# A kernel of four graph layers: q copied to PSUM a block ahead, and layer 0's count of places read one step later

## The chip, the cores and the metric

The kernel runs on one core of one Trainium2 chip. The core has a matrix engine (TensorE, "PE" in the profile; its weight loads are "PEld"), a vector engine (VectorE, "DVE"), a scalar engine (ScalarE, "ACT"), a general engine (GpSimd, "POOL"), a queue engine (SyncE, "SP") and 16 DMA engines. Each engine runs its own instructions in order and waits for others by semaphores. Tiles lie in SBUF, or in PSUM, which the matrix engine writes.

The metric is the device time of one execution in microseconds (us). Several runs are taken, and their median counts.

## The reference, cut to what matters

There are 3327 nodes with 256 features and a 0/1 matrix `adj` of 3327 x 3327, which is sparse: an entry is 1 with probability 0.0048, so that a node has some 16 neighbours. Layer 0 weighs neighbours and the others with a softmax whose scores take only two values in a row. Layers 1 to 3 are attention over the neighbours, each followed by an MLP.

```python
# layer 0
h = x @ Wt.T + bt                                  # 64 features
s = leaky_relu(h @ Wa.T + ba, negative_slope=0.2)
w = softmax(where(adj > 0, s, NEG), axis=1)
y = x + (w @ h) @ Wp.T + bp
x = gamma * (y - mean(y)) * rsqrt(var(y) + EPS) + beta

# layers 1, 2, 3
qkv = layer_norm(x, g1, be1) @ w_qkv               # q, k, v: 8 heads of 32
scores = einsum("nhd,mhd->hnm", q, k) * SCALE
attn = softmax(where(adj != 0, scores, -inf), axis=-1)
x = x + einsum("hnm,mhd->nhd", attn, v).reshape(n, 256) @ w_proj + b_proj
x = x + gelu(layer_norm(x, g2, be2) @ w1 + b1) @ w2 + b2
```

## The kernel before

**Layer 0** goes over `adj` in 26 blocks of 128 rows. Per block it loads the rows, takes the sign (ACT), turns them with PE (ACT copies the turned tiles out of PSUM), sums the neighbours' features with PE, and finds the list of neighbours of each row with DVE (`candidates`, `list`). Rows come in groups of four blocks. When a group's sums are there, its steps run spread over the following blocks: `soft`, then `mix`, `project` and so on.

The kernel sorts the nodes by their degree. For this, `soft` makes a one-hot row `OH` of each node's degree and lets PE count, into the PSUM tile `places`, how many earlier nodes have the same degree; DVE reads the count back into `rank`:

```python
def soft(self):
    ...                                            # deg from the group's sums
    nc.vector.tensor_tensor(OH[:, b0:b0 + n, :], ..., ALU.is_equal)
    at = places[:, :4 * nd].rearrange("p (b k) -> p b k", k=nd)
    for j in range(n):
        ...
        nc.tensor.matmul(at[:, j, :], lhsT, OH[:, m, :], start=False, stop=True, ...)
    t = aw.tile([P, 4, nd], FP, tag="place", ...)
    nc.vector.tensor_mul(t, at[:, :n, :], OH[:, b0:b0 + n, :])          # L906
    nc.vector.tensor_reduce(rank[:, b0:b0 + n], t, AX.X, ALU.add)       # L907
    if b0 + n == NB:
        nc.tensor.matmul(at[:, n - 1, :], rest_tri, OH[:, NB - 1, :], ...)
        S.all = at[:, n - 1, :]
    ...                                            # twelve small DVE operations
    nc.scalar.activation(m1, m1, AF.Exp)
    nc.scalar.activation(m0, m0, AF.Exp)

def mix(self):
    ...                                            # uses m1, m0; ten DVE operations
    nc.vector.tensor_add(nb, nb, t3)
```

After `soft` of a group, `list` of the current block follows, and `mix` comes at the start of the next block, before its `candidates`.

**Layers 1 to 3** work on the sorted nodes, again 26 blocks of 128. `CAPS[b]` is the most neighbours that a node of block `b` may have (40 down to 10). The blocks are taken in the order 25, 1, 24, 2, ..., 12, 13, 0. The neighbours of a block are gathered in groups of four (`GS = 4`): for each of the four, one indirect DMA brings the k and v rows of 128 nodes to a tile of a ring of ten (`kv`, L1298, issued by POOL). DVE multiplies k by q and sums over each head (`scores`), takes softmax, and multiplies v by the weights (`vw`, L1361); PE sums these over the neighbours in PSUM (`po`, L1366). A tile of the ring is free again after its `vw`.

```python
q2 = ps_q.tile([P, 2, D], FP, name="q2")           # PSUM; D = 256, float32

def take_q(self, b):
    self.q[b] = q2[:, ORDER.index(b) % 2, :]
    nc.scalar.copy(self.q[b], t2[:, b, D:2 * D])                        # L1306

def scores(self, b, s0):
    ...
    nc.vector.tensor_mul(k, k, self.q[b][:, None, :].to_broadcast(...)) # L1320
    nc.vector.tensor_reduce(self.sc[b][:, s0:s0 + n, :], ..., ALU.add)  # L1321
    if L == 1:
        nc.scalar.copy(t2[...], t[:, :n, 2 * D])                        # L1324

def softmax(self, b):
    nc.vector.tensor_tensor_reduce(sc, sc, pad[b]..., mx)               # L1332
    nc.scalar.activation(sc, sc, AF.Exp, bias=mx, scale=-1.0)           # L1335
```

The rest of a layer is cut in small steps, which `some()` issues one or a few at a time between the groups. `short` steps finish a block: copy `o`, turn it, copy `oT` (L1396), project (PE, L1402), add to the row (`t`, DVE, L1406) and its statistics. `long` steps work on a chunk of up to four blocks: norm (DVE, then ACT L588, PE L591, ACT L596), the MLP's `up` (PE, L1445), `gelu` (ACT, L1451) and `down` (PE, L1468), `shift` (ACT, L1474), turning back (PE, L1482), add (DVE, L1486), and in layers 1 and 2 the next layer's q, k and v (PE, L1498), copied out by ACT (`kvr`, L1504, and `t`, L1505).

```python
self.take_q(ORDER[0])
for k, b in enumerate(ORDER):
    for g in slots[b]:                             # the groups of block b
        self.scores(*g)
        if g == slots[b][-1]:
            self.softmax(b)
            if k + 1 < NB:
                self.take_q(ORDER[k + 1])
        for i in wait:
            wait[i] += 1
        for _ in range(2 if len(todo) > NBUF // 2 or b == 0 else 1):
            if todo and wait[todo[0][0]] > 1:
                value()                            # weights once per block; vw; po
        self.some()
    todo += slots[b]
    wait[b] = 0
```

The weights and values of a block thus begin two groups after its softmax.

Of the kernel before, what the change touches and what calls it, by code (L numbers as in the profile page):

```python
# [8 lines left out]
FP = mybir.dt.float32  # L9
# [3 lines left out]
ALU = mybir.AluOpType  # L13
AX = mybir.AxisListType
# [3 lines left out]
P = 128  # L18
# [14 lines left out]
NB = (N + P - 1) // P  # L33
# [490 lines left out]
def sparse_path(ctx, tc, ins, out, dram, flag):  # L524
    nc = tc.nc
# [13 lines left out]
    rank = const.tile([P, NB], FP, name="rank")  # L539
# [83 lines left out]
    with tc.tile_pool(name="a", bufs=1) as a, tc.tile_pool(name="aw", bufs=2) as aw, \  # L623
# [45 lines left out]
        for name, n in (("gamma", D), ("beta", D), ("bt", H0), ("Wa", H0), ("ba", 1)):  # L669
# [10 lines left out]
        nd = LMAX + 1  # L680
# [3 lines left out]
        OH = a.tile([P, NB, nd], BF, name="OH")  # L684
        rest_tri = a.tile([P, P], BF, name="rest_tri")
        nc.vector.tensor_sub(rest_tri, ones_bf, tri)

        places = a_acc.tile([P, 512], FP, tag="places", name="places")
# [3 lines left out]
                         skip_group_check=True)  # L692
# [148 lines left out]
        class Group:  # L841
# [36 lines left out]
            def soft(self):  # L878


                g, n, b0 = self.g, self.n, self.blocks[0]

                def sv(name):
                    t = aw.tile([P, 4], FP, tag="s_" + name, bufs=1, name=f"s_{name}_{g}")
                    return t[:, :n]

                sg = S.s[:, b0:b0 + n]
                dg = deg[:, b0:b0 + n]
                nc.vector.tensor_copy(dg, self.acc[:, :n, H0])
                top = sv("top")  # L890
                nc.vector.tensor_scalar(top, dg, float(LMAX), None, ALU.min)
                nc.vector.tensor_tensor(OH[:, b0:b0 + n, :],
                                        num[:, None, :nd].to_broadcast([P, n, nd]),
                                        top[:, :, None].to_broadcast([P, n, nd]), ALU.is_equal)

                at = places[:, :4 * nd].rearrange("p (b k) -> p b k", k=nd)
                for j in range(n):
                    i = b0 + j
                    add = [(tri, i)] + [(ones_bf, k) for k in range(b0, i)]
                    if g:  # L900
                        add += [(rest_tri, i - 4)] + [(ones_bf, k) for k in range(i - 3, b0)]
                    for lhsT, m in add:
                        nc.tensor.matmul(at[:, j, :], lhsT, OH[:, m, :], start=False, stop=True,
                                         skip_group_check=True)
                t = aw.tile([P, 4, nd], FP, tag="place", bufs=1, name=f"place_{g}")[:, :n]
                nc.vector.tensor_mul(t, at[:, :n, :], OH[:, b0:b0 + n, :])  # L906
                nc.vector.tensor_reduce(rank[:, b0:b0 + n], t, AX.X, ALU.add)  # L907
                if b0 + n == NB:
                    nc.tensor.matmul(at[:, n - 1, :], rest_tri, OH[:, NB - 1, :], start=False,
                                     stop=True, skip_group_check=True)  # L910
                    S.all = at[:, n - 1, :]
                non, ga, fa, m1, m0, tt, mx = (
                    sv(k) for k in ("non", "ga", "fa", "m1", "m0", "tt", "mx"))
                nc.vector.tensor_scalar(non, dg, -1.0, float(N), ALU.mult, ALU.add)
                nc.vector.tensor_scalar(ga, dg, 0.0, None, ALU.is_gt)
                nc.vector.tensor_scalar(fa, non, 0.0, None, ALU.is_gt)
                nc.vector.tensor_scalar(tt, ga, -NEG0, NEG0, ALU.mult, ALU.add)
                nc.vector.tensor_mul(m1, sg, ga)
                nc.vector.tensor_add(m1, m1, tt)
                nc.vector.tensor_scalar(tt, fa, -1.0, 1.0, ALU.mult, ALU.add)  # L920
                nc.vector.tensor_mul(m0, sg, tt)
                nc.vector.scalar_tensor_tensor(m0, fa, NEG0, m0, ALU.mult, ALU.add)
                nc.vector.tensor_max(mx, m1, m0)
                nc.vector.tensor_sub(m1, m1, mx)
                nc.vector.tensor_sub(m0, m0, mx)
                nc.scalar.activation(m1, m1, AF.Exp)
                nc.scalar.activation(m0, m0, AF.Exp)
                self.non, self.m1, self.m0, self.tt = non, m1, m0, tt

            def mix(self):  # L930
                g, n, b0, acc = self.g, self.n, self.blocks[0], self.acc
                m1, m0, tt = self.m1, self.m0, self.tt
                z = aw.tile([P, 4], FP, tag="s_z", bufs=1, name=f"s_z_{g}")[:, :n]
                nc.vector.tensor_mul(z, deg[:, b0:b0 + n], m1)
                nc.vector.tensor_mul(tt, self.non, m0)
                nc.vector.tensor_add(z, z, tt)
                nc.vector.reciprocal(z, z)
                nc.vector.tensor_mul(m1, m1, z)
                nc.vector.tensor_mul(m0, m0, z)
                shape = [P, n, H0]  # L940
                nb = self.nb = aw.tile([P, 4, H0], FP, tag="nb", bufs=1, name=f"s_nb_{g}")[:, :n]
                t3 = aw.tile([P, 4, H0], FP, tag="t3", bufs=1, name=f"s_t3_{g}")[:, :n]
                nc.vector.tensor_sub(t3, S.hsum[:, None, :].to_broadcast(shape), acc[:, :n, :H0])
                nc.vector.tensor_mul(t3, t3, m0[:, :, None].to_broadcast(shape))
                nc.vector.tensor_mul(nb, acc[:, :n, :H0], m1[:, :, None].to_broadcast(shape))
                nc.vector.tensor_add(nb, nb, t3)

            def project(self):
                g, n = self.g, self.n
                pt = bank(f"s_ptn_{g}")  # L950
                for j in range(n):
                    nc.tensor.transpose(pt[:H0, j * P:(j + 1) * P], self.nb[:, j, :], ident)
                nc.scalar.copy(S.nT[:H0, :n * P], pt[:H0, :n * P])
                self.ps = []
                for j0 in range(0, n, 2):
                    ps = bank(f"s_pp_{g}_{j0}").rearrange("p (b d) -> p b d", d=D)
                    for j in range(2):
                        nc.tensor.matmul(ps[:, j, :], S.nT[:, (j0 + j) * P:(j0 + j + 1) * P], S.wpT,
                                         start=True, stop=True)
                    self.ps.append(ps)  # L960
# [120 lines left out]
        for g in reversed(range(NG)):  # L1081
            at = dict(zip(names, (0, 1, 3, 4, 5, 6, 7, 8, 9, 10, 11, 12)))
# [11 lines left out]
            for name in names:  # L1094
                k = first + at[name]
# [39 lines left out]
        t = aw.tile([P, NB, nd], FP, tag="v", name="t_more")  # L1135
# [36 lines left out]
        for i in range(NB):  # L1172
            nc.tensor.matmul(pp[:, :2 * NB], oh_lo[:, i, :],
                             ids[:, i, :, :].rearrange("p a b -> p (a b)"),
                             start=(i == 0), stop=(i == NB - 1))
# [87 lines left out]
    ORDER = [b for k in range(NB // 2) for b in (NB - 1 - k, k + 1)][:NB - 1] + [0]  # L1263
    CHUNK, at = {}, 0
# [5 lines left out]
    slots = {b: [(b, s) for s in range(0, CAPS[b], GS)] for b in ORDER}  # L1270

    class Layer:
# [289 lines left out]
        def run(self):  # L1562
            for _ in range(NBUF):
                self.issue()
            self.take_q(ORDER[0])

            todo, wait = [], {}

            def value():
                if todo[0][1] == 0:  # L1570
                    self.weights(todo[0][0])
                self.values(*todo.pop(0))

            for k, b in enumerate(ORDER):
                for g in slots[b]:
                    self.scores(*g)
                    if g == slots[b][-1]:
                        self.softmax(b)
                        if k + 1 < NB:
                            self.take_q(ORDER[k + 1])  # L1580
                    for i in wait:
                        wait[i] += 1
                    for _ in range(2 if len(todo) > NBUF // 2 or b == 0 else 1):
                        if todo and wait[todo[0][0]] > 1:
                            value()
# [3 lines that stand above are left out]
            while todo:  # L1589
                value()  # L1590
                self.some()
            self.rate = 4.0
            while self.short or self.long:
                self.some()
# [45 lines left out]
```

## Time and profile before

The median of three runs is 2787.56 us (2777.72 to 2789.45). The profiled execution has a span of 2779.3 us, and PE was granted 0.836 of its full clock on the mean.

| engine | busy us | share of the span | instructions |
|---|---|---|---|
| PE | 1952.0 | 70% | 6409 |
| PEld | 1045.3 | 38% | 6409 |
| DVE | 1961.9 | 71% | 4061 |
| ACT | 806.5 | 29% | 1398 |
| POOL | 1361.8 | 49% | 1458 |

Layer 0 ends near 525 us, where the first gather of layer 1 is issued. The gathers of layer 1 are issued from 525.0 to 1179.7 us, those of layer 2 from 1303.5 to 1952.5, those of layer 3 from 2074.6 to 2683.3. POOL issues one of them every 1.25 us when it waits for nothing (0.95 us busy, 0.30 between).

A line of the list of waits names who waited, at which line of the kernel and for which tile, then the engine, tile and line that released it, then the total of the waits, their number and the longest. A line of the timeline gives the start and length of an instruction, its engine and line, what it writes and reads, and in brackets how long the engine had been idle before it and what ended that.

### The profile page before, as it was taken

The numbers are of one execution on the slowest core, as the hardware profiler recorded it, in microseconds if no ns is written. First come the engines' busy times: TensorE is split into PE (matmuls) and PEld (weight loads), VectorE is DVE, ScalarE is ACT, GpSimd is POOL, SyncE is SP. The second block draws the span as 40 slices with busy tenths as digits, with TensorE's granted clock in tenths as the row PEclk, the third lists the DMA queues.
The fourth block names the chain that finished last, engine by engine and source line by source line (L and its number), as shares of the span: only waits on it lengthen the run. The fifth ranks groups of instructions, "written<-read, shape, count | busy, mean of one in ns | idle before, by whom it ended". The sixth has DMA issues, their size and how long they took to land. (4 is left out here: it accounts for less than half of the span.)

```text
span 2779.3 us, 21889 instructions
## 1 busy us (share of the span) xinstructions
PE 1952.0 (70%) x6409; PEld 1045.3 (38%) x6409; DVE 1961.9 (71%) x4061; ACT 806.5 (29%) x1398; POOL 1361.8 (49%) x1458
## 2 busy tenths in 40 slices
PE   5657665248788887884377887887853678867866
PEld 4546553114333333442133443433431333333334
DVE  6597888577877777733788677778427878778852
ACT  5346552102332322321022332232320222222221
POOL 4000000377766666601776565566017777776741
PEclk9768776678899898897788898898976898988988
DMA  6224420677766666613776565566227766666650
GB/s 235 99 106 154 155 81 32 198 217 217 222 196 200 202 182 186 182 34 100 209 211 201 168 195 180 158 190 178 50 70 210 210 183 199 201 190 184 198 130 15
DMA packets 144478, 453.66 MB, mean 163 GB/s; under 512 B 29521, under 2 KB 40156, under 8 KB 141021
## 3 DMA queue, kind: packets, MB, share of 16 engines
q0 software_dynamic: 113056, 370.26, 46.0%
q1 hardware_dynamic: 9834, 53.90, 5.5%
q10 hardware_dynamic: 21458, 28.02, 2.9%
q8 instruction: 52, 0.85, 0.1%
q14 instruction: 78, 0.64, 0.1%
HBM read 420.64 MB, written 31.42 MB: 163 GB/s over the span
## 5 line engine op out<-in xcount | busy, mean ns | idle before, releaser
L1298 POOL DMA_INDIRECT kv<-kv,t x1344 | 1272.8, 947 | 810.0 <-issue 350.4
L1366 PE MATMUL po<-vw,s_ident 128*128 128x512 f32 (+1 forms) x1380 | 770.4, 694 | 497.4 <-DVE vw L1361 447.6
L1320 DVE TENSOR_TENSOR kv<-kv,q 128x1024 f32<-128x1024 f32 (+3 forms) x363 | 413.3, 1139 | 312.6 <-ACT q L1306 156.5
L1366 PEld LDWEIGHTS po<-vw,s_ident 128*128 128x128 f32 x1380 | 285.3, 220 | 846.5 <-issue 468.3
L1321 DVE TENSOR_REDUCE sc<-kv 128x32 f32<-128x1024 f32 (+3 forms) x363 | 414.1, 1141 | 12.4
L1361 DVE TENSOR_TENSOR vw<-kv,w 128x1024 f32<-128x1024 f32 x333 | 371.3, 1127 | 0.2
L1445 PE MATMUL pu<-fT,s_w 128*128 128x512 f32 (+3 forms) x768 | 308.1, 536 | 1.0 <-ACT fT L596 1.0
L1468 PE MATMUL py<-gT,s_w 128*128 128x512 f32 (+2 forms) x672 | 283.4, 549 | 0.0
L1451 ACT ACTIVATE gT<-pu,pvb 128x512 f32<-128x512 f32 (+3 forms) x192 | 116.4, 607 | 361.0 <-PE pu L1445 360.7
L1445 PEld LDWEIGHTS pu<-fT,s_w 128*128 128x128 f32 x768 | 150.6, 206 | 140.5 <-issue 116.0
L711 POOL MEMSET s_abf<- 128x1 bf16 x23 | 2.2, 105 | 375.2 <-DVE s_v L731 248.3
L1468 PEld LDWEIGHTS py<-gT,s_w 128*128 128x128 f32 x672 | 127.6, 191 | 122.0 <-issue 104.4
L723 PE MATMUL s_ptb<-s_ident_bf,s_abf 128*128 128x128 bf16 x676 | 69.8, 273 | 77.3 <-ACT s_abf L714 64.0
L735 DVE MAX8 cand<-s_v 128x8 f32<-128x208 bf16 x416 | 118.0, 359 | 0.9
L588 ACT ACTIVATE xn_f<-t,nm_f,rqy_f 128x256 f32<-128x256 f32 x78 | 42.9, 593 | 247.5 <-DVE nm_f L582 240.1
L1498 PE MATMUL pk<-s_w_qkv,nT 128*128 128x512 f32 x208 | 104.4, 626 | 8.9 <-ACT nT L596 8.9
L1335 ACT ACTIVATE sc<-sc,mx 128x120 f32<-128x120 f32 (+6 forms) x78 | 32.0, 410 | 259.8 <-DVE mx L1332 259.2
L1406 DVE TENSOR_TENSOR t<-t,po 128x256 f32<-128x256 f32 x78 | 32.5, 417 | 103.8 <-PE po L1402 97.9
L1486 DVE TENSOR_TENSOR t<-t,pd 128x256 f32<-128x256 f32 x75 | 29.5, 408 | 91.0 <-PE pd L1482 91.0
L723 PEld LDWEIGHTS <-s_abf 128*128 128x128 bf16 x676 | 58.8, 125 | 91.8 <-ACT s_abf L714 70.8
L855 PE MATMUL s_pa<-s_aT,s_hs 128*128 128x256 bf16 x338 | 80.4, 286 | 13.2 <-DVE s_hs L817 13.2
L724 ACT COPY s_aT<-s_ptb 128x896 bf16<-128x896 bf16 x104 | 82.7, 859 | 19.9 <-PE s_ptb L723 19.7
(292 smaller groups left out, 2343.5 us busy)
## 6 DMA issues: line engine op xcount, KB each, us to landing
s_a<-in_adj_dram SPq DMA_DIRECT2D x25, 1663.5 KB
kv<-kv,t POOLq DMA_INDIRECT x1344, 3.7
kv<-kvr ACTq DMA_DIRECT2D x52, 256.0 KB
kv<-s_kvr ACTq DMA_DIRECT2D x26, 256.0 KB
s_w<-in_L_gnn_w_dram SPq DMA_DIRECT2D x6, 1024.0 KB
t<-ql ACTq DMA_DIRECT2D x6, 592.0 KB
t<-s_x ACTq DMA_DIRECT2D x6, 512.0 KB
s_w_qkv<-in_L_gnn_w_qkv_dram SPq DMA_DIRECT2D x3, 768.0 KB
```

Source lines behind the costliest of these rows:

```text
L723: nc.tensor.transpose(pt[:, m, :], self.abf[:, k * P:(k + 1) * P], ident_bf)
L724: nc.scalar.copy(aT[:, k0:k0 + len(ks), :], pt[:, :len(ks), :])
L735: nc.vector.max(out=self.cand[:, s, :], in_=self.v[:, s, :])
L1298: nc.gpsimd.indirect_dma_start(out=t[:, s, :], out_offset=None, in_=kv[L], in_offset=bass.IndirectOffsetOnAxis(ap=t2[:, b, k:k + 1].bitcas ...
L1320: nc.vector.tensor_mul(k, k, self.q[b][:, None, :].to_broadcast([P, n, D]))
L1321: nc.vector.tensor_reduce(self.sc[b][:, s0:s0 + n, :], k.rearrange("p s (h d) -> p s h d", d=HD), AX.X, ALU.add)
L1361: nc.vector.tensor_mul(vw[:, :n * D].rearrange("p (s h d) -> p s h d", h=HEADS, d=HD), v, self.wp[b][:, s0:s0 + n, :, None].to_broadcast([ ...
L1366: nc.tensor.matmul(self.po[b][:, :m], ident, vw[:, s * D:s * D + m], start=(s0 + s == 0), stop=(s0 + s + 2 >= S), skip_group_check=True)
L1445: nc.tensor.matmul(c["pu", f][:, :n], w["w1"][:, e, f * P:(f + 1) * P], c["hT"][:, e, :n], start=(e == 0), stop=(e == 1))
L1451: nc.scalar.activation(g[:, :n], c.pop(("pu", f))[:, :n], AF.Gelu_apprx_tanh, bias=w["b1"][:, f:f + 1])
L1468: nc.tensor.matmul(c["py"][e][:, :n], w["w2"][:, f, e * P:(e + 1) * P], g[:, :n], start=(f == 0), stop=last)
L1498: nc.tensor.matmul(ps[:, :c1 - c0], c["hT"][:, e, j * P:(j + 1) * P], nxt["w_qkv"][:, e, c0:c1], start=(e == 0), stop=(e == 1))
```

## The change

Two things move; no operation is added or taken away.

The copy of the next block's q to PSUM stood after the softmax of the current block. It now stands before the second group of the current block. q2 has two halves, which blocks use in turn, so that the copy for the next block goes to the half that the current block doesn't read. The aim is that q is there long before the next block's first group.

In layer 0, reading the count of places, with the last block's extra matmul, moves from `soft` to the end of `mix`. The aim is that DVE does other work while PE counts.

```diff
@@ soft
-                t = aw.tile([P, 4, nd], FP, tag="place", bufs=1, name=f"place_{g}")[:, :n]
-                nc.vector.tensor_mul(t, at[:, :n, :], OH[:, b0:b0 + n, :])
-                nc.vector.tensor_reduce(rank[:, b0:b0 + n], t, AX.X, ALU.add)
-                if b0 + n == NB:
-                    nc.tensor.matmul(at[:, n - 1, :], rest_tri, OH[:, NB - 1, :], start=False,
-                                     stop=True, skip_group_check=True)
-                    S.all = at[:, n - 1, :]
@@ a new step
+            def place(self):
+                g, n, b0 = self.g, self.n, self.blocks[0]
+                at = places[:, :4 * nd].rearrange("p (b k) -> p b k", k=nd)
+                ...                                # the lines taken out of soft
@@ mix
                 nc.vector.tensor_add(nb, nb, t3)
+                self.place()
@@ run
             for k, b in enumerate(ORDER):
                 for g in slots[b]:
+                    if g == slots[b][1] and k + 1 < NB:
+                        self.take_q(ORDER[k + 1])
                     self.scores(*g)
                     if g == slots[b][-1]:
                         self.softmax(b)
-                        if k + 1 < NB:
-                            self.take_q(ORDER[k + 1])
```

More of the change, by code (lines that the diff above doesn't have):

```diff
@@ L928, in soft @@
                 self.non, self.m1, self.m0, self.tt = non, m1, m0, tt
+            def place(self):
+                g, n, b0 = self.g, self.n, self.blocks[0]
+                at = places[:, :4 * nd].rearrange("p (b k) -> p b k", k=nd)
+                t = aw.tile([P, 4, nd], FP, tag="place", bufs=1, name=f"place_{g}")[:, :n]
+                nc.vector.tensor_mul(t, at[:, :n, :], OH[:, b0:b0 + n, :])
+                nc.vector.tensor_reduce(rank[:, b0:b0 + n], t, AX.X, ALU.add)
+                if b0 + n == NB:
+                    nc.tensor.matmul(at[:, n - 1, :], rest_tri, OH[:, NB - 1, :], start=False,
+                                     stop=True, skip_group_check=True)
+                    S.all = at[:, n - 1, :]
             def mix(self):
```

## The prediction, made before the changed kernel ran

> **What bounds the kernel now.** I read the chain of waits first. Its shares add up to under 10% of the span, so it covers too little to rank stages, and I went on to the list of all waits, then to the stretches where the waits in question lie. Of the list of waits (who waits, for whom; us in total, times, longest) these rows carry the case:
>
> ```profile
> PE po L1366 <- DVE vw L1361: 447.6, 137, 35.0
> ...
> DVE kv L1320 <- ACT q L1306: 156.5, 42, 7.3
> DVE kv L1320 <- DMA kv<-kv,t: 147.0, 67, 6.9
> ...
> POOL kv L1298 <- DVE vw L1361: 102.4, 43, 9.4
> ...
> DVE place L906 <- PE places L903: 41.1, 7, 16.2
> ```
>
> VectorE (DVE) waits 156.5 us for the copy of q and 41.1 us for the count of places. These are the two waits that the change attacks. Whether they are worth anything is a question of stage, so I asked for busy time by stretch (length, then each engine's busy us):
>
> ```profile
> 100.00:300.00 200.00, 131.99 (x886) 102.97 (x884) 148.95 (x542) 108.76 (x130) 1.01 (x10) 0.74 0.36 127
> 300.00:460.00 160.00, 109.47 (x744) 83.10 (x742) 141.35 (x520) 79.38 (x106) 3.68 (x9) 0.78 0.31 102
> 1591.00:1693.00 102.00, 83.25 (x215) 39.34 (x215) 76.41 (x132) 30.28 (x52) 62.03 (x66) 0.90 0.59 177
> ```
>
> Layer 0 (first two rows; columns PE, PEld, DVE, ACT, POOL): from 100 to 460 us DVE is busy 290 of 360 us, and its gaps above 0.25 us there add up to 59 us, 41 of them the wait for places. DVE sets the pace of that stage. Layers 1 and 2 (third row, one turn of four blocks in layer 2): PE 83, DVE 76, POOL 62 of 102 us. No engine is full. DVE works while PE is short of work, then PE works through a backlog (MLP and next layer's qkv) while DVE waits; the turn is the sum of both phases. Layer 3 has turns of 92 us, as it has no qkv.
>
> How one such wait arises (timeline of layer 2, block 19's first group; start, length, engine, line):
>
> ```profile
> 1590.23 0.36 ACT L1306 COPY q<-t 128x256 f32<-128x256 f32 x1
> ...
> 1590.62 1.22 DVE L1320 TENSOR_TENSOR kv<-kv,q 128x1024 f32<-128x1024 f32 x1 [5.95 <-ACT q L1306]
> ...
> 1593.02 0.41 DVE L1406 TENSOR_TENSOR t<-t,po 128x256 f32<-128x256 f32 x1
> ...
> 1594.10 1.22 DVE L1320 TENSOR_TENSOR kv<-kv,q 128x1024 f32<-128x1024 f32 x1
> ...
> 1597.16 0.39 ACT L1505 ACTIVATE t<-pq 128x256 f32<-128x256 f32 x1 [0.28 <-PE pq L1498]
> ...
> 1599.03 0.94 POOL L1298 DMA_INDIRECT kv<-kv,t  x1 [9.39 <-DVE vw L1361]
> ```
>
> The copy takes 0.36 us; the 5.95 us before it is ScalarE (ACT) being late, since everything it runs in order waits for PE's backlog (that list: ACT gT waits 360.7 us for PE pu). So q is a place where DVE is tied to ACT, and the question is where the tie lies afterwards.
>
> **What the skill says.** "PSUM — Partial Sum Buffer", section "PSUM bank collisions raise a hardware error": two engines must not touch one bank in the same partitions at once, even at different addresses, so PSUM is to be guarded by bank. Its specification gives 2 KiB per bank. q2 is 2 x 256 float32, 2048 bytes: both halves are in one bank. In the instruction order of the built kernel this is what stands: ACT's copy for the next block now waits for the multiply of the current block's first group, and the multiply of its second group waits for that copy, though it reads the other half. The same page, "Engine vs sequencer instructions": the queues of ScalarE and VectorE are strictly first in, first out. The trace agrees (ACT runs the copy only after all that was written ahead of it). "ScalarE activation tables: per-element evaluation and per-set limits", section "What a function is on this engine", has a table load at 1283 ns; the trace shows 1.28 us, twice around each exp that stands between gelus.
>
> **The change part by part, layers 1 to 3.** No instruction is added or removed; 75 copies of q move ahead. What DVE no longer waits for: at the first group of a block, the exp, its table load and the copy. What it now waits for: at the second group, the copy, and with it all that ACT has ahead of it, including what the first group's turn issued (gelu, kvr, q of the next layer), each waiting for PE. Before, those were not needed at that point. So the tie moves about one group later for DVE and about one turn of side work later for ACT.
>
> Block 19 above. After the change the first multiply starts when DVE is free, near 1584.7, and its product is done at 1587.2. L1406 still waits for PE's projection, which ends at 1591.97; statistics until 1593.1. The second multiply could then start at 1593.1, but ACT's last instruction ahead of the copy is the L1505 that ends at 1597.55. Plus 0.36 for the copy and some 0.06 to be seen: 1597.97, against 1594.10 before. So 3.9 us later, not 5.95 earlier. Nothing makes PE's qkv end sooner. From 1594 to 1629 DVE has 1 us of gaps in all, so the 3.9 us goes through to the next norm (its last step at 1617.76), for which PE is waiting (3.2 us idle at 1615.44), and so to the start of the next MLP.
>
> Read the same way (end of ACT's last instruction ahead of the copy's new place, plus 0.42, less the start of the second group's multiply now), blocks 21, 19, 17, 15, 13 give 0.8, 3.8, 4.2, 4.6, 4.9 in layer 1 (18.3) and 1.2, 3.9, 4.3, 4.7, 4.9 in layer 2 (19.0).
>
> Blocks 20, 18, 16, 14 lie in the MLP phase: 3.5 us each by the same reading (block 18: gelu ends 1643.06, multiply at 1639.97). There PE is busy without a gap. The value product delayed by it (1643.41, done at 1648.1 then) is wanted by PE at 1647.26, so PE loses 0.9 us each: 3.6 per layer. The first turn: block 22 comes 2.6 later and costs PE 2.0; at block 4 the multiply (1461.35) must wait for the shift that ends at 1466.36, so 5.4 later, and a value product behind it stands ahead of the turning-back of that chunk on PE, which is critical. Together about 6 per layer.
>
> Blocks 23, 5, 7, 9, 11 and 6, 8, 10, 12 lose nothing and gain nothing: the first five did not wait, and in the last four a wait for PE's projection follows (6.07 us at 1664.18) that takes the gain over.
>
> Layers 1 and 2: 18.3 + 19.0 + 2 x 3.6 + 2 x 6 = 56.5 us longer. Layer 3: there is no kvr ahead of the copy, blocks 18, 16, 14 give 1.7 each, in front of a gather wait of 2 to 4 us each turn that takes it over; at 19, 17, 15 DVE may gain 0.9. I put 0.
>
> **Layer 0.** The multiply and sum of places (0.33 + 0.32 us) move behind 12 small operations (1.9 us), the list (3.7 us) and the mix (2.4 us), 8 us in all, in a stage set by DVE. The seven waits are 16.2, 1.0, 13.6, 4.1, 3.1, 2.6 and 0.6 us. Each is covered up to 8 us: 8 + 1.0 + 8 + 4.1 + 3.1 + 2.6 + 0.5 = 27. The exp that the mix needs stands in ACT ahead of PE's long sums (ACT was free at 242.1, PE's counts were done at 247.4), so no new wait of that size arises. I take 3 off as the next wait for PE meets an earlier DVE: 24 us shorter.
>
> Sum: 2787.6 + 56.5 - 24 = 2820. As a few of the delays may be taken up by PE's gaps (PE waits 447.6 us for DVE in all, but the tails of the layers wait for gathers), I take a little off: 2816.
>
> **The rivals.** First, the wait disappears, as the change intends: DVE drops 156.5 us. For it: 6 to 9 us POOL stalls stand right beside the 6 us waits in layers 1 and 2 (9.39 at 1599.03). POOL's cadence of 1.25 us per gather puts a layer's 448 gathers at 559 us against 655, 649 and 609 us from first to last, so 60 to 90 us per layer would be there to be had: some 2660 to 2700. Against it: the wait in the built order at the second group, and that ACT is late because of PE, not because of the exp. Second, the tie moves and costs nothing, since gathers or PE set the pace: then only layer 0 counts, 2764. For it: POOL busy 0.6 to 0.7 in the layers; against it: DVE has hardly any gather wait between 660 and 1180 us and between 1435 and 1920. Third, all delays add without cover (the 3.5 of the MLP blocks too): 18.3 + 19 + 28 (8 x 3.5) + 12 + 6 (layer 3) - 10 (a smaller gain in layer 0) = 73, 2861.
>
> **Range and chances.** The layers may give 25 to 85, layer 0 from -30 to -10; the runs of before spread by 12 us. 2785 to 2848 should hold it 8 times in 10. Faster by 2% (under 2731.8) needs the first rival: 0.04. Slower by 2% (over 2843.3): 0.15. Within: 0.81.
>
> **What would show it.** In the changed profile: the row of DVE waiting for q still over 120 us, now before second groups, at 17 to 19 blocks of layers 1 and 2 and up to 5 us or more each; turns of layer 2 near 107 us instead of 103; layer 3's near 92; POOL's wait for vw above 102; the wait for places near 14 us in two instances, and layer 0 over 20 to 27 us sooner (the first gather of kv near 501 instead of 525.0). I am wrong if the q row falls under 60 us, if PE's qkv phase starts earlier in a turn, or if layer 0 keeps its length because PE takes over the pace.

## The result, and the profile after

The changed kernel took 2825.02 us (median of four runs, 2821.68 to 2825.86), and the kernel before 2785.89 beside it: a ratio of 1.0142, with an interval of 1.0118 to 1.0167. It is 39 us slower. The profiled execution has a span of 2822.7 us and a mean granted clock of 0.831 (0.836 before).

The code below the moved lines stands five lines further down: L1320 of before (multiply by q) is L1325 now, L1306 (copy of q) is L1311, L1361 (vw) is L1366, L1406 (add to the row) is L1411.

The list of waits of the changed kernel (who waits, for whom; us in total, times, longest):

```profile
PE po L1371 <- DVE vw L1366: 492.3, 156, 35.1
...
DVE t L1411 <- PE po L1407: 172.3, 41, 7.8
DVE kv L1325 <- DMA kv<-kv,t: 161.1, 76, 7.1
...
POOL kv L1303 <- DVE vw L1366: 131.2, 41, 15.2
...
DVE kv L1325 <- ACT q L1311: 89.0, 25, 5.7
...
ACT q L1311 <- DVE kv L1325: 64.0, 31, 13.6
...
DVE t L1411 <- ACT q L1311: 47.8, 8, 6.4
...
DVE place L927 <- PE places L903: 5.5, 2, 2.8
```

The wait for places fell from 41.1 to 5.5 us, and the wait for q from 156.5 to 89.0. But another row grew: VectorE's sum at the end of a block waits 172.3 us for PE's projection, plus the 47.8 us that the list puts down to ACT's q. That second row is the same wait: the sum reads nothing of q, and at all eight places it starts 0.11 us after the projection's last matmul, as it does where the list names the projection. Together they are 220 us, where before it was 97.9 + 5.8 = 104:

```profile
DVE t L1406 <- PE po L1402: 97.9, 36, 6.6
...
DVE t L1406 <- ACT q L1306: 5.8, 2, 3.9
```

And there is a row that before had no counterpart: ScalarE's copy waits 64.0 us for VectorE's multiply.

The same place as in the prediction, layer 2, block 19 (start, length, engine and line, in brackets the idle time before and what ended it):

```profile
1608.45 1.21 DVE L1325 TENSOR_TENSOR kv<-kv,q 128x1024 f32<-128x1024 f32 x1
...
1617.87 0.42 DVE L1411 TENSOR_TENSOR t<-t,po 128x256 f32<-128x256 f32 x1 [6.96 <-PE po L1407]
...
1622.96 0.38 ACT L1510 ACTIVATE t<-pq 128x256 f32<-128x256 f32 x1 [0.28 <-PE pq L1503]
...
1623.39 0.38 ACT L1311 COPY q<-t 128x256 f32<-128x256 f32 x1
...
1623.80 1.22 DVE L1325 TENSOR_TENSOR kv<-kv,q 128x1024 f32<-128x1024 f32 x1 [4.82 <-ACT q L1311]
...
1628.50 3.35 PE L1371 MATMUL po<-vw,s_ident 128*128 128x512 f32 x4 [3.00 <-DVE vw L1366]
1628.72 0.94 POOL L1303 DMA_INDIRECT kv<-kv,t  x1 [15.22 <-DVE vw L1366]
```

The tie has moved. The first group's multiply (1608.45) waits for nothing now. VectorE gets to the sum earlier and waits 6.96 us there for PE; before, the 5.95 us of waiting for q stood ahead of the sum and covered that wait. Then the second group's multiply waits 4.82 us more for q of the *next* block, which ScalarE copies only after its queue of copies for the next layer's qkv. Behind it PE idles 3.00 us, and POOL has stood still for 15.22 us (9.39 before).

Busy time by stretch for the changed kernel (length, then PE, PEld, DVE, ACT and POOL busy us, clock, DMA share, GB/s): one turn of layer 2, from block 19's first multiply to block 17's, then layer 0.

```profile
1608.45:1714.77 106.32, 86.04 (x217) 40.01 (x216) 76.60 (x134) 31.25 (x52) 61.34 (x65) 0.89 0.58 170
100.00:300.00 200.00, 139.89 (x971) 108.73 (x970) 156.34 (x566) 112.81 (x136) 1.12 (x11) 0.75 0.40 139
300.00:444.00 144.00, 99.69 (x681) 74.98 (x679) 134.83 (x500) 75.83 (x100) 3.58 (x8) 0.78 0.30 102
```

The same two multiplies of before stand at 1590.62 and here:

```profile
1693.14 1.22 DVE L1320 TENSOR_TENSOR kv<-kv,q 128x1024 f32<-128x1024 f32 x1 [6.10 <-ACT q L1306]
```

So this turn grew from 102.5 to 106.3 us with VectorE's work unchanged (76.8 and 76.6 us). In layer 0 VectorE did its 291 us of work in 344 us instead of 360. By the first gather of each layer and the end of the span, the stages are:

| stage | before, us | after, us | difference | predicted |
|---|---|---|---|---|
| layer 0, to the first gather | 525.0 | 509.0 | -16.0 | -24 |
| layer 1 | 778.5 | 806.0 | +27.5 | +27.9 |
| layer 2 | 771.1 | 802.4 | +31.3 | +28.6 |
| layer 3 to the end | 704.7 | 705.3 | +0.6 | 0 |

### The profile page after: what moved, and what is told of

Read it like the earlier page. It is cut to its first block, busy times and chain, and to the rows that moved or that the text cites. A ratio compares the mean times of both kernels' runs of the same rounds, so it can differ in the third digit from the quotient of the medians.

```text
span 2822.7 us, 21943 instructions
## 1 busy us (share of the span) xinstructions
PE 1969.7 (70%) x6409; PEld 1044.3 (37%) x6409; DVE 1958.8 (69%) x4061; ACT 811.4 (29%) x1398; POOL 1364.2 (48%) x1458
## 5 line engine op out<-in xcount | busy, mean ns | idle before, releaser
L1371 PE MATMUL po<-vw,s_ident 128*128 128x512 f32 (+1 forms) x1380 | 784.1, 704 | 542.6 <-DVE vw L1366 492.3
L1325 DVE TENSOR_TENSOR kv<-kv,q 128x1024 f32<-128x1024 f32 (+3 forms) x363 | 412.7, 1137 | 257.0 <-DMA kv<-kv,t 161.1
L1366 DVE TENSOR_TENSOR vw<-kv,w 128x1024 f32<-128x1024 f32 x333 | 371.2, 1127 | 0.3
L1411 DVE TENSOR_TENSOR t<-t,po 128x256 f32<-128x256 f32 x78 | 32.6, 418 | 221.6 <-PE po L1407 172.3
L855 PE MATMUL s_pa<-s_aT,s_hs 128*128 128x256 bf16 x338 | 81.9, 289 | 13.2 <-DVE s_hs L817 13.2
L588 ACT ACTIVATE xn_n<-t,nm_n,rqy_n 128x256 f32<-128x256 f32 x52 | 28.6, 593 | 206.8 <-DVE nm_n L582 182.0
```

The source lines that it names most:

```text
L855: nc.tensor.matmul(self.pa[:, c0:c0 + 2 * P], S.hs[:r, k, :P], aT[:r, k, :], start=(k == 0), stop=(k == NB - 1))
L1366: nc.vector.tensor_mul(vw[:, :n * D].rearrange("p (s h d) -> p s h d", h=HEADS, d=HD), v, self.wp[b][:, s0:s0 + n, :, None].to_broadcast([ ...
L1371: nc.tensor.matmul(self.po[b][:, :m], ident, vw[:, s * D:s * D + m], start=(s0 + s == 0), stop=(s0 + s + 2 >= S), skip_group_check=True)
```

## The experiments

My theory: the copy of q, moved ahead, ties VectorE and ScalarE through the PSUM bank that both halves of q2 share, and costs some 57 us in layers 1 and 2; the place change gives back 24. The rivals: the loss comes from layer 0's new order, or from the copy's new place in ScalarE's order and not from the bank, or from ScalarE held up and not VectorE; and the wait for q, once really gone, might be worth its time. The first four kernels ran beside a kernel before of 2781.31 us, the next four beside one of 2776.94.

**Each part alone.** Before, with only one of the two moves.

```diff
  e1_q_ahead_only: before, and in run
+                    if g == slots[b][1] and k + 1 < NB:
+                        self.take_q(ORDER[k + 1])
                     self.scores(*g)
                     if g == slots[b][-1]:
                         self.softmax(b)
-                        if k + 1 < NB:
-                            self.take_q(ORDER[k + 1])
  e2_place_only: before, and place() taken out of soft and called at the end of mix
```

> The kernel before with the move of q's copy alone; layer 0 untouched. Theory (the tie of VectorE to ScalarE moves to the second group, and there waits for ScalarE's whole backlog): layers 1 and 2 are each some 28 to 31 us longer, layer 3 unchanged, layer 0's end at 525 us as before: 2786 + 59 = 2845 us, ratio 1.021. Rival (part of the loss comes from layer 0's new order, which shifts where the layers start): under 2835.

> The kernel before with the later reading of the count of places alone. Theory: the first gather comes at 506 to 509 us instead of 525, and the layers keep their lengths: 2786 - 18 = 2768 us, ratio 0.9935. Rival (layer 0's gain is given back in layer 1): 2780 or more.

Measured: q ahead alone 2844.46 us, ratio 1.0218 (1.0184 to 1.0252); places alone 2763.13, ratio 0.9927 (0.9908 to 0.9946). The two multiply to 1.0143, against 1.0142 for both: the parts don't touch each other. The first costs 63 us, the second gives 18. The waits of the first look like those of the changed kernel (q 79.2 us in 23, projection 162.0 + 47.7).

**The bank.** The same move, with q and the weights w regrouped so that the two blocks in turn use two banks, at the same 4 KB per partition; and the regrouping alone, with the copy where it was.

```diff
  e3_two_banks_ahead: e1, and
-    q2 = ps_q.tile([P, 2, D], FP, name="q2")
-    w2 = ps_q.tile([P, 2, D], FP, name="w2")
+    qw = [ps_q.tile([P, 2, D], FP, name=f"qw{k}") for k in range(2)]
-            self.q[b] = q2[:, ORDER.index(b) % 2, :]
+            self.q[b] = qw[ORDER.index(b) % 2][:, 0, :]
-                wp = w2[:, ORDER.index(b) % 2, :S * HEADS]
+                wp = qw[1 - ORDER.index(b) % 2][:, 1, :S * HEADS]
  e4_two_banks_alone: before, and these lines without the move
```

> q's copy before the second group as in the changed kernel, layer 0 as before, but the two halves of q2 in two different PSUM banks (each shared with a half of w2), so that the multiply of the second group no longer waits for the copy. Theory: the 59 us of the change vanish; but the waits for q before were mostly cover of the wait for PE's projection that follows them, so hardly anything is gained against the kernel before: 2775 to 2788 us, ratio 0.996 to 1.001, with the row of the sum t waiting for PE's projection risen from 98 to 170 us or more. Rival (the wait for q was worth its 156 us and only the shared bank spoiled the change): 2680 to 2730 us. Second rival (the bank isn't what matters, the copy's place in ScalarE's order is): 2835 or more.

> The two banks alone: q's copy at its old place after the softmax. All theories: as the kernel before within 0.3% (2778 to 2794 us), with the wait for q again near 156 us. Were it faster or slower by more, the new layout of PSUM would itself cost or give time, and the run with two banks and q ahead would have to be read against this one.

Measured: with the move 2776.29 us, ratio 0.9975 (0.9963 to 0.9987); without it 2781.19, ratio 1.000 (0.9985 to 1.0014). So the layout by itself is worth nothing (VectorE waits 144.7 us for q in it, 156.5 before), and the move that costs 63 us in one bank gains 5 in two. The Trainium skill ("PSUM — Partial Sum Buffer", section "PSUM bank collisions raise a hardware error") says that it is the bank that counts and not the address: two engines collide in one bank, in the same partitions, even at different addresses. The trace agrees as to what waits for what: the two kernels with the move differ only in which half lies in which bank, and are 68 us apart, with 79.2 and 2.4 us of waiting for q. VectorE's rows in the list of waits of the first of the two (here q is in qw, and the lines are L1405, L1319 and L1305):

```profile
DVE t L1405 <- PE po L1401: 163.5, 39, 8.7
DVE kv L1319 <- DMA kv<-kv,t: 159.7, 77, 7.2
...
DVE t L1405 <- ACT qw L1305: 66.4, 8, 8.6
...
DVE kv L1319 <- ACT qw L1305: 2.4, 1, 2.4
```

The wait for q is gone: 2.4 us in place of 156.5. The wait for the projection has taken its place, 163.5 + 66.4 = 230 us where it was 104. Of 154 us less in one row, 126 came back in the next. The new layout has a tie of its own: ScalarE's copy waits 77.1 us, at 18 places, for VectorE's vw, whose weights share a bank with q. The timeline of this kernel, at the block shown above:

```profile
1590.24 0.42 DVE L1405 TENSOR_TENSOR t<-t,po 128x256 f32<-128x256 f32 x1 [5.20 <-PE po L1401]
...
1591.34 1.22 DVE L1319 TENSOR_TENSOR kv<-kv,qw 128x1024 f32<-128x1024 f32 x1
```

The second group's multiply starts right after the sum and its statistics, 1.1 us later, as the copy isn't waited for (it stands at 1595.76 on ScalarE). But the sum itself comes 2.8 us earlier than the 1593.02 of before, of which 1.7 us is that layer 2 began so much sooner here. In this place the hoped-for gain is 1 us of 5.95.

**Which of the two ties costs.** The shared bank makes two: VectorE waits for the copy, and the copy waits for VectorE's first multiply. I put each back by itself into the kernel with two banks, through a column of one element per partition.

```diff
  e5_tie_vector: e3, and after take_q
+                        nc.scalar.copy(tie, ident[:, 0:1])
+                        nc.vector.tensor_copy(tied, tie)
  e6_tie_scalar: e3, and after take_q
+                        nc.scalar.copy(tie, self.tiles[slots[b][0]][:, 0, 0:1])
```

> Two banks and q ahead (2776 us), and one half of the tie put back without q: at the copy's new place ScalarE writes a column of 128 numbers, and VectorE copies that column before the multiply of the second group. VectorE waits for ScalarE's backlog there, ScalarE doesn't wait for VectorE. Some 0.2 us each of added work, 75 times, most of it in gaps. Theory (the loss is VectorE's wait for what ScalarE has queued ahead of that place): the loss of the change comes back, 2776 + 59 + 0 to 10 = 2835 to 2845 us. Rival (the loss is ScalarE held up behind a copy that waits for VectorE): 2776 to 2790 us.

> Two banks and q ahead (2776 us), and the other half of the tie: at the copy's new place ScalarE reads a column of the first group's product, so that it waits for VectorE's multiply of that group, while VectorE waits for nothing of it. Theory: 2772 to 2786 us, since ScalarE waits in any case for the matrix engine next. Rival (ScalarE held up costs the time; it waited 64 us for that multiply in the changed kernel): 2810 or more.

Measured: with VectorE tied 2852.29 us, ratio 1.0267 (1.0239 to 1.0296); with ScalarE tied 2771.93, ratio 0.998 (0.9964 to 0.9995). The list of waits with VectorE tied:

```profile
DVE t L1405 <- PE po L1401: 220.7, 49, 8.6
...
DVE tied L1580 <- ACT tie L1578: 96.6, 29, 5.8
```

The loss of the one-bank kernel is VectorE waiting for the copy. That the copy waits costs nothing that shows, though ScalarE waited only 40.2 us for the tied column (16 times), against 64.0 in the changed kernel. With VectorE tied, layers 1 and 2 took 814.8 and 803.2 us, close to the 812.2 and 797.6 of q ahead in one bank. The direction is clear and the size is 7 to 17 us over what I expected. VectorE's 75 added copies take up to 75 x 0.144 = 11 us by themselves, so the tie alone has no clean number from this.

**Both kept.** Two banks, q ahead and the place change, that is, the changed kernel with its fault taken out.

```diff
  e7_two_banks_and_place: the changed kernel, and
-    q2 = ps_q.tile([P, 2, D], FP, name="q2")
-    w2 = ps_q.tile([P, 2, D], FP, name="w2")
+    qw = [ps_q.tile([P, 2, D], FP, name=f"qw{k}") for k in range(2)]
     ...                                            # take_q and wp as in e3
```

> The changed kernel with the two halves of q2 in two banks: both moves without the tie. If the parts add up: 2776 - 18 = 2758 us, ratio to the kernel before 0.991. More than 2766 would mean that the earlier start of layer 1 is given back in it.

Measured: 2747.92 us, ratio 0.9905 (0.9876 to 0.9935). This beats both kernels; by stage 505.1 us to the first gather, then 768.5, 764.4 and 704.8. The product of the two parts alone, 0.9927 x 0.9975 = 0.9902, says the same.

**The wait that came after.** If the wait for the projection has taken over, moving the sum back in VectorE's order should give the hidden gain. One empty step more ahead of `add`:

```diff
  e8_add_later: e7, and in the short steps of a block
-            return [lambda: None, copy, lambda: None, fold, turn, copy_T, project, lambda: None, add]
+            return [lambda: None, copy, lambda: None, fold, turn, copy_T, project, lambda: None,
+                    lambda: None, add]
```

> As the run with two banks and place (2758 us), and the addition of the projection to the row one side-work step later, so that the second group's multiply no longer stands behind VectorE's wait for the matrix engine's projection. Theory (with the tie gone, that wait is what took over the wait for q, and VectorE's next products are what the gathers and the matrix engine wait for): 2700 to 2745 us, with the wait of the sum t under 150 us (230 us with two banks alone). Rival (the turn is set by the matrix engine's backlog, whichever instruction VectorE waits at): 2750 to 2765 us.

Measured: 2741.41 us, ratio 0.9887 (0.9857 to 0.9917). The time is in the expected range, but the mark isn't: the wait for the projection is 213.6 us (52 times), not under 150, and the interval overlaps with that of the kernel without the step. In the trace the added step takes the sum behind the second group's multiply in every other block only. This settles nothing, for or against.

The last four kernels ran on another chip, where the kernel before took 3276.43 us, and where layers 1 to 3 have idle stretches that no profile of the first chip shows; they are compared with each other and with that kernel only.

**The sum two steps later.** As in e8, with two empty steps in place of one.

```diff
  e9_add_a_turn_later: e7, and in the short steps of a block
-            return [lambda: None, copy, lambda: None, fold, turn, copy_T, project, lambda: None, add]
+            return [lambda: None, copy, lambda: None, fold, turn, copy_T, project, lambda: None,
+                    lambda: None, lambda: None, add]
```

> As two banks and place (2748 us), with two empty steps ahead of the addition instead of the one of the last run, so that the second group's multiply and sum (2.4 us) stand ahead of VectorE's wait for the projection in every block; with one empty step they did in every other block only. Theory (the turn is set by the matrix engine's backlog, wherever VectorE waits): 2735 to 2750 us again, with the wait of the sum t still over 150 us. Rival (VectorE's waiting there is lost time of the turn): some 40 blocks times 2.4 us less, 2650 to 2700 us.

Measured: 3090.04 us, ratio 0.943 (0.9401 to 0.946). The nearest kernel without the two steps on that chip is e12_place_in_project below, 3233.83 us, 144 us above it. So there that wait is worth more than the theory allowed, and by the time the rival has it. By its mark the theory has it: the wait for the projection is still 161.0 us, though it was 254.4 in e12. But that wait is itself longer there (up to 26.6 us for the projection in the kernel without the steps, 6.8 in e7 on the first chip). How much of the gain would be left on the first chip wasn't measured, and whether this wait is what hides the gain of q there stays open.

**The copy one group later still.** Before, with take_q ahead of the third group, in one bank.

```diff
  e10_third_group: before, and in run
+                    if g == slots[b][2] and k + 1 < NB:
+                        self.take_q(ORDER[k + 1])
                     self.scores(*g)
                     if g == slots[b][-1]:
                         self.softmax(b)
-                        if k + 1 < NB:
-                            self.take_q(ORDER[k + 1])
```

> The kernel before with q's copy before the third group instead of the second, both halves in one bank as before. Read from the trace of before as the prediction read it (end of ScalarE's last instruction ahead of the copy, plus 0.42, less the start of the third group's multiply): 19, 17, 15, 13 lose 1.8 to 2.9 us, 5, 7, 9, 11 now lose 5 us each (a copy of po stands ahead), 22 loses 5; layer 3 has losses too, up to 3 us in eight blocks. Theory: 33 to 36 us in each of layers 1 and 2, 5 to 20 in layer 3, together 2777 + 70 to 90 = 2847 to 2867 us. Rival (a tie later in the block is looser, as ScalarE has had more time): 2780 to 2815 us.

Measured: 3231.33 us, ratio 0.9876 (0.9826 to 0.9925): faster, where I expected 70 to 90 us slower. VectorE's waits there:

```profile
DVE t L1406 <- PE po L1402: 319.1, 41, 25.2
DVE kv L1320 <- ACT q L1306: 200.2, 33, 20.3
```

Waits of 20 and 25 us occur in no such row of the first chip (longest 7.6 and 8.8 in any kernel there). The delay worked out from the one chip's timeline didn't carry over to the other, and this run can't judge the reading. It is a miss, and stays open.

**PE's part of the turn.** e7 with half of the matmuls of `up` left out, so that only half of its sum is computed.

```diff
  e11_half_up: e7, and in up
-                for e in range(2):
+                for e in range(1):
                     nc.tensor.matmul(c["pu", f][:, :n], w["w1"][:, e, f * P:(f + 1) * P],
-                                     c["hT"][:, e, :n], start=(e == 0), stop=(e == 1))
+                                     c["hT"][:, e, :n], start=True, stop=True)
```

> As two banks and place (2748 us), but the MLP's first product sums over half of its 256 inputs only (half of the matmuls of up left out; nothing of VectorE's, ScalarE's or the gathers' work changes in size). That takes 16 of the 0.43 us matmul records from a chunk of four blocks, 6.9 us of the matrix engine's work in each turn, some 42 us in a layer. Theory (in layers 1 and 2 the matrix engine's backlog sets the second half of a turn): 60 to 90 us less in all, 2658 to 2688 us, with layer 3 much less changed, since gathers take over there. Rival (VectorE's own chain sets the turn, the matrix engine has room): 2735 or more.

Measured: 3156.14 us, ratio 0.9641 (0.9617 to 0.9665), 78 us under e12_place_in_project (which also differs in layer 0, by some 5 us). From first to last gather layers 1 to 3 took 782.9, 756.9 and 726.0 us against 806.2, 780.0 and 747.7: about 23 us less in each; with what follows the last gather the layers are 34, 34 and 27 us shorter. The sum is of the size expected, but I had expected layer 3 to change little, and it changed nearly as much. That PE's backlog sets part of each turn holds there; that layer 3, which has no qkv in its turns, is free of it doesn't.

**The places read later still.** e7 with `place()` at the start of project.

```diff
  e12_place_in_project: e7, and
                 nc.vector.tensor_add(nb, nb, t3)
-                self.place()
 
             def project(self):
                 g, n = self.g, self.n
+                self.place()
```

> As two banks and place (2748 us), with the count of places read one step later still, at the start of project. In the changed kernel two waits for the count of 2.8 and 2.7 us are left, and the waits for ScalarE's exp (4.4 and 3.3) stay. Theory: the first gather 4 to 6 us earlier, 2742 to 2744 us, within the runs' spread. Rival (the matrix engine or ScalarE sets layer 0 by now): no earlier.

Measured: 3233.83 us, ratio 0.9873 (0.9827 to 0.9918). The first gather comes at 505.9 us, against 511.3 and 510.5 in the two kernels of the same chip that read the places at the end of mix, and 527.4 in the one that reads them in soft: 5 us sooner, as much as I expected. This isn't shown, though: it is one profile of each, and on the first chip the first gather of kernels with the same layer 0 spreads by as much (522.1 to 527.0, and 503.7 to 509.0). No wait for the count is left in it, but the next wait for PE, that for layer 0's projection, is 11.2 us, against 6.9 in the two others. The idle stretches of this chip, by its list of waits:

```profile
DVE o L1391 <- ACT o L1388: 258.9, 19, 25.7
...
ACT gT L1455 <- remote: 166.7, 11, 29.0
```

The second row names "remote" as what ended 11 idle stretches of up to 29.0 us. Other rows there name it too, up to 32.5 us; no row of any profile of the first chip does. What it is I can't tell.

## Why the prediction was right

- **The tie moves, and is not removed.** Right, and shown: with the halves in two banks the loss is gone, with VectorE tied again it is back, with ScalarE tied it isn't. The first rival (the wait disappears, 2660 to 2700 us) is out even with two banks: then the wait for q does disappear, for 5 us, as the wait for PE's projection behind it takes over. The second rival (the tie costs nothing) is out by the 63 us of q ahead alone, the third (all delays add, some 83 us in the layers) by the 59.4 that they grew.
- **Blocks 21 to 13.** The second group's multiply was to come 3.8, 4.2 and 4.6 us later at blocks 19, 17 and 15 of layer 1. After the start of PE's qkv phase it came 6.5 us later in before, and 10.3, 10.7 and 11.1 us later in the changed kernel: 3.8, 4.2 and 4.6. In layer 2 the four turns from block 21 to block 13, by that multiply, took 411.4 us before and 433.1 now: 21.7 more, where the parts read off before add up to 3.9 + 4.3 + 4.7 + 4.9 + 4 x 0.9 = 21.4. "Near 107 instead of 103" was 108.3 against 102.9 in the mean. In layer 1 the same four turns took 410.6 and 427.3 us: 16.7 more, where the parts add up to 21.1. Single turns don't fit: those of layer 2 grew by 9.6, 2.7, 7.8 and 1.6 us.
- **Layers 1 and 2 together.** 58.8 us measured, 56.5 predicted. That they are so close is in part luck: from the first gather to block 21's second multiply the two layers grew by 8.3 and 8.5 us, where 6.8 and 7.2 were predicted (the first turn and block 21), and behind block 13 by 2.6 and 1.1, where nothing was, which makes up for layer 1's four turns. The 0.9 us of the MLP blocks weren't measured by themselves; VectorE's waits there were read rightly (3.5 us; 3.3 measured at seven of the eight places, none at the eighth). One reading of the path was off: the 3.2 us that PE idles at 1615.44 in before end with a value product (L1366) and not with the norm. VectorE's delay reaches both.
- **Layer 3.** 0 predicted, 0.6 measured.
- **Layer 0: the term that was mis-sized.** 24 us predicted, 16.0 in this profile. The six profiles of the first chip with the places read in soft have their first gather at 522.1 to 527.0 us (mean 524.8), the four with the new place at 503.7 to 509.0 (mean 506.0): 19 us. The two large waits kept 13.2 us together, as the 14 that I had foreseen, but only 5.5 of it is for places. The timeline of VectorE in the changed kernel, at the first of the two:

```profile
130.73 0.16 DVE L938 TENSOR_TENSOR s_z<-deg,s_m 128x4 f32<-128x4 f32 x1 [4.39 <-ACT s_m L919]
...
136.10 0.33 DVE L927 TENSOR_TENSOR place<-places,OH 128x164 f32<-128x164 f32 x1 [2.84 <-PE places L903]
136.46 0.32 DVE L928 TENSOR_REDUCE rank<-place 128x4 f32<-128x164 f32 x1
```

  I had written that the exp would bring no new wait of that size; the mix waits 4.39 us for it here and 7.7 us in all. But this only stands in for the wait for places, and the cover came out as worked out: 41.1 - 5.5 - 7.7 = 27.9 us against 27. What was too small is the 3 us that I took off since VectorE, being earlier, meets the next wait for another engine: layer 0's projection (`s_pp`, from PE) is 6.9 us, new; the product for h (`s_ph`, from PE) 15.7 instead of 12.8; the sum of the neighbours (`deg`) 6.0 instead of 4.7; the norm's row (`s_x`, from ScalarE) 7.4 instead of 6.2. Together 12.3 us, and 27.9 - 12.3 = 15.6, where the stage shows 16.0. Of the four only `s_pp` is sure: it stands at 6.8 to 6.9 us in all four profiles of the first chip with the new place and in none without. The others vary between kernels with the same layer 0: `s_ph` is 12.8 to 15.8 us without the new place and 9.6 to 15.7 with it.
- **The shading from 2820 to 2816.** I took 4 us off for delays that PE's gaps might absorb. None shows: layers 1 and 2 came out 2.3 us over the unshaded sum. The 28.4 us that I had given, 4.1 for the shading, 2.3 and 0.6 for the layers and 8.0 for layer 0 make 43.4 us, the difference of the two profiled executions. The medians differ by 39 us: the profiled execution of before, 2781.14 us, was faster than its median.
- **The mark of the q row.** Over 120 us predicted, 89.0 measured, at 25 places: 21 second groups of layers 1 and 2 (the blocks that the prediction names make 22, and not 17 to 19), three of layer 3 and the first group of all. The waits themselves were read rightly: at block 19, 1597.97 - 1593.1 = 4.9 us, where 4.82 was measured. But the 120 wasn't worked out from them. Eight blocks with 4.9 (19 to 13, two layers), eight with 3.5 (20 to 14), and twice 2.6 + 5.4 for the first turn make 39 + 28 + 16 = 83. The rest of the old 156.5 us is in the wait for the projection, which VectorE now meets earlier and first. A row's total is a poor mark for this reason, since the beginning of a wait decides in which row it is counted; the mean length of the turns was a good one.
- **POOL's wait for vw.** Above 102 predicted, 131.2 measured.

## What to carry to other kernels

Two halves of one PSUM bank are no double buffer between two engines: here the writer of one half and the reader of the other took turns, and a copy moved ahead to save a wait cost 63 us until the halves lay in two banks. Before taking a wait away, read what the same engine waits for next in its queue: 154 us of waits for q turned into 126 us more of waits for PE's projection, and 5 us of time. And to foresee where a moved tie bites, take the end of the producer's last instruction ahead of it in the new order, plus its own length, less the start of the consumer, and then judge what other engines' waits take over of it. Here this gave 56.5 us where 58.8 were measured, with parts that were off by up to 4.4 us; used for another place of the copy, on another chip, it had the sign wrong.

## What was not expected of the hardware

- The same kernel took 3276.43 us on one chip and 2776.94 to 2785.89 on another, 18% apart. Layer 0 is as long on both (first gather at 527.4 us against 522.1 to 527.0), and so is VectorE's work (1957.1 us busy in e12_place_in_project, 1958.8 in the changed kernel); layers 1 to 3, which gather their neighbours by indirect DMA, stretch. PE's granted clock is lower there (0.787 in e12_place_in_project, 0.838 in e7), and PE is busy 99 us longer, of the 486 us between these two. What causes the rest is open.
- A row of the list of waits can name the wrong engine: 47.8 us (66.4 with two banks) that VectorE's sum spent waiting for PE stand as a wait for ScalarE's copy of q, which the sum doesn't read.
- At block 19 of layer 2 in the changed kernel PE's first four qkv matmuls took 3.73 us where the next four of the same shape took 1.88; this alone made the delay there 5.6 us instead of 3.9. The granted clock was 0.51 from 1611.76 to 1615.40 us and 1.00 right after; at the same place of before (1587.70 to 1589.60) it was 1.00. So the clock, too, had a part in the length of this turn.
